# Two-pass quantised self-attention in a four-block network: where its first queries are levelled, what its shifts are formed from, and a bias for its exponentials

## The chip, the cores and the metric

The kernel runs on one core of a Trainium2 chip. A core has five engines that run side by side, each with its own instruction queue: TensorE (PE, matrix products and transposes into PSUM), VectorE (DVE), ScalarE (ACT, the activation functions), GpSimd (POOL) and SyncE (SP, which here only issues DMA). Engines wait for each other by semaphores; each works its queue in order. The metric is the device time of one execution in microseconds (us), as a median over runs.

## The reference

The network maps `x` (4096 tokens of 288 channels, here 32 tiles of 128 tokens, in 4 batches of 1024) through four blocks in a chain: block 0, a transformer block with 8-bit quantised linear layers; block 1, a cross-attention; block 2, a transformer block with fake-quantised attention; block 3, of block 0's kind. The change is mostly in block 2:

```python
def _fake_quant(x, n_bits, always_zero=False):
    levels = float(2 ** n_bits - 1)
    if always_zero:
        delta = jnp.max(x) / levels
        zp = 0.0
    else:
        xmin, xmax = jnp.min(x), jnp.max(x)
        delta = (xmax - xmin) / levels
        zp = jnp.round(-xmin / delta)
    xq = jnp.clip(_ste_round(x / delta) + zp, 0.0, levels)
    return (xq - zp) * delta

def _quant_attention(x, ctx, Wq, Wk, Wv, Wo, bo):
    q, k, v = (heads(a) for a in (x @ Wq, ctx @ Wk, ctx @ Wv))
    q, k, v = (_fake_quant(a, 8) for a in (q, k, v))
    probs = softmax(einsum('bhqd,bhkd->bhqk', q, k) / sqrt(HD))
    probs = _fake_quant(probs, 8, always_zero=True)
    return merge(einsum('bhqk,bhkd->bqhd', probs, v)) @ Wo + bo

n1 = _ln(h, ln1_g, ln1_b)
h = h + _quant_attention(n1, n1, Wq1, Wk1, Wv1, Wo1, bo1)
```

There are 16 heads of HD = 18. The minima and maxima in `_fake_quant` run over the whole tensor, all batches and heads included, so every query, key and value must exist before one of them can be quantised, and every probability before one of them can be.

## The kernel before

`x` stays on chip through all four blocks. Block 2 is `fq_attn` (L2864), which runs in four stages.

**Projection.** For each of 32 token tiles, LayerNorm (partly on POOL, lines L148 and L149), transposes, and the product with the joined Wq, Wk, Wv on TensorE (L2643, L2644); ScalarE copies the 864 results out as `y` (L3012), VectorE takes their extremes (`min_max`, L812 and L813), and `y` goes to DRAM as `raw`. In the same loop `context` prepares the keys and values of the block's cross-attention (`kq`, kT, kv, kbd), interleaved with the tiles. Then the extremes over everything become a step, its reciprocal, a zero point and a top for each of query, key and value: `global_params` (L784), called for `kq` here, for `gq` at the end of the projection, and for `qq` in the tail. Its one step across partitions is a `partition_all_reduce` on POOL (L793). `verdict` (L1201) at the end of the program and `prob_params` (L822) hold one each too.

**Pass 1** (`fq_passes`, L3030). Queries and keys are read back from `raw` (`fetch`), turned into integer levels (`fq_levels`, L819 and L820), placed with padding (`place`, L3086) and transposed on TensorE and copied by ScalarE to `qk` (`operands`, L3119). All this for batch 0 is done first: keys by VectorE, queries by POOL (`first_queries`, L3088), which runs a tile ahead of need. The loop runs over batches, head groups of four, eight query tiles and two pairs of heads: two score tiles of 128 queries x 1024 keys in PSUM (`scores_pair`, L3747), an exponential of each with its row sum (L3194, into `sums`), and one VectorE maximum over both (L3201, into `top`). The exponentials' factor is a register, `rstep`. Four tiles `e` go round between ScalarE and VectorE. Meanwhile POOL makes the levels of the next batch (`levels`, L3098). After each batch `largest` (L3148) forms 1/sums (`r`) and the largest probability of each row.

**Between the passes.** `prob_params` gives `pd`, the probabilities' step. A probability's level is exp(score) / (sums x pd), so the kernel shifts every score by -ln(sums x pd). It forms y = sums x pd (L3221), z = ln y (L3222), u = exp(-z) (L3227), and (1 - u y - z) / step, which corrects z's error once, and splits it in three bf16 parts (`log_shifts`, L3224). `add_shift` (L2541) copies a tile's parts into spare columns (POOL, L2545), transposes them (L2551), and adds them to the queries' padding rows (VectorE, L2552), where the keys hold ones. The work between the passes is in the order in which it stands in the code: 128 columns of parts, the four shifts of the first half batch, then the other 384 columns.

**Pass 2** (`attend_levels`, L3756). For 4 batches x 2 halves x 4 head groups x 8 key tiles: four score products (L3787) of keys spread block-wise in `kz` (two buffers, loaded by DMA), two exponentials of 128 x 1024 (L3796), one VectorE rounding of both to bf16 (`eb`, L3802) and four products with the values (L3770). `beside_half` weaves the output product with Wo, the next LayerNorms, the cross-attention's queries and the next half's shifts into it.

Behind it `fq_tail` does the cross-attention (its queries come back from `rawq` as `qn`) and the feed-forward. Block 3 follows; the last thing in it are `ff_stage` (L2427) and `level_residual` (L1865), whose last lines decide the program's end:

```python
y = self.wk.tile([P, C], F32, tag="y", name="y", bufs=2)
nc.vector.scalar_tensor_tensor(y, ps[:, :C], sc[:, j : j + 1], w["sw"], ALU.mult, ALU.mult)
...
nc.gpsimd.tensor_tensor(self.x[:, t, :], self.x[:, t, :], y, ALU.add)
```

Each sum of x is then stored by a DMA from SP (L2485). Along the way the kernel collects flags for values outside the range it can handle (`watch_range`, L1220); `verdict` takes the largest of them, loads it to a register, and a slower general program would run if it were not zero.

The scheduler keeps each engine's instructions nearly in the order of the code, save where `tc.issue_after(...)` sets something behind another instruction. Pools give out on-chip memory in turn, so a tile may wait until the one that lay there has been read.

Of the kernel before, what the change touches and what calls it, by code (L numbers as in the profile page):

```python
# [28 lines left out]
F32 = mybir.dt.float32  # L29
F32R = mybir.dt.float32r  # L30
BF16 = mybir.dt.bfloat16
# [6 lines left out]
P = 128  # L38
B, S, C, H, D, T, FF = 4, 1024, 288, 16, 18, 64, 1152
NTB = S // P  # L40
# [1140 lines left out]
class Fast(Net):  # L1181
# [19 lines left out]
    def verdict(self):  # L1201

        nc = self.nc
        s = self.cp.tile([P, 1], F32, name="bads")
        nc.vector.tensor_reduce(s, self.bad, AX.X, ALU.max)
        al = self.cp.tile([P, 1], F32, name="bada")
        nc.gpsimd.partition_all_reduce(al, s, P, bass_isa.ReduceOp.max)
        fl = self.cp.tile([1, 1], mybir.dt.int32, name="badi")
        nc.vector.tensor_copy(fl, al[0:1, :])
        return nc.values_load(fl[0:1, 0:1])  # L1210

    @contextmanager
# [651 lines left out]

    def level_residual(self, qT, sc, w, t, j, bias=None):  # L1865

        nc = self.nc
        ps = self.ps1()
        self.mm(ps[:, :C], qT[:, :, j * P : (j + 1) * P], w["T"], 0, C)
        y = self.wk.tile([P, C], F32, tag="y", name="y", bufs=2)  # L1870
        nc.vector.scalar_tensor_tensor(y, ps[:, :C], sc[:, j : j + 1], w["sw"], ALU.mult, ALU.mult)
        if bias is not None:
            nc.vector.tensor_tensor(y, y, bias, ALU.add)  # L1873
        nc.gpsimd.tensor_tensor(self.x[:, t, :], self.x[:, t, :], y, ALU.add)  # L1874

# [551 lines left out]
    def ff_stage(self, g3, b3, w1, w2, tops, out, m, nb, wide):  # L2427
# [5 lines left out]
        def tokens(t0):  # L2433
# [47 lines left out]
            for j in range(m):  # L2481
                t = t0 + j
                self.level_residual(fT, fc, w2, t, j)
                if out is not None:
                    nc.sync.dma_start(out[t * P : (t + 1) * P, :], x[:, t, :])  # L2485
                yield "p1.1 d.5 g.8", 0 if j + 1 < m else None
# [54 lines left out]
    def add_shift(self, qT, sp, parts, t):  # L2541


        nc = self.nc
        nc.gpsimd.tensor_copy(  # L2545
            sp[:, :, D : D + 3], parts[:, :, t * H : (t + 1) * H].rearrange("p k h -> p h k")
        )
        ps = self.ps1(BF16)
# [315 lines left out]
    def fq_attn(self, w, ctxT, beside):  # L2864
# [10 lines left out]
        with ExitStack() as es:  # L2875
# [96 lines left out]
            with (  # L2972
# [44 lines left out]
                while side:  # L3017
                    aside()
            q = self.global_params(gp, mx, nmn, "gq")

            self.watch_range(-0.5, 255.5, q["zp"], "zext")

# [7 lines left out]
    def fq_passes(self, w, q, step, raw, rawq, qmx, qmn, side, aside):  # L3030

        tc, nc = self.tc, self.nc
        with ExitStack() as es:
# [6 lines left out]
            v = gp.tile([P, NT, C + HP - D], BF16, name="v")  # L3040
            nc.gpsimd.memset(v[:, :, C:], 0.0)

            kzs = [gp.tile([P, 2, S], BF16, name="kz0")]
            spads = [gp.tile([P, H, HP], BF16, name=f"spad{n}") for n in range(2)]
# [10 lines left out]
            tp = tops.enter_context(tc.tile_pool(name="f1m", bufs=1))  # L3055
            top = tp.tile([P, NT, H], F32, name="top")
            sums = tp.tile([P, NT, H], F32, name="sums")
            r = tp.tile([P, NT, H], F32, name="rs")
            tmx = tp.tile([P, B], F32, name="tmx")
            with (  # L3060
                tc.tile_pool(name="f1l", bufs=3) as ld,
# [9 lines left out]

                def fetch(b, n, j0, m):

                    y = ld.tile([P, 3 * C], F32, tag="in", name="in")
                    y = y[:, : m * C].rearrange("p (m c) -> p m c", m=m)
                    nc.sync.dma_start(y, raw[b][:, j0 : j0 + m, n * C : (n + 1) * C])
                    return y

                def place(b, n, j, y, eng):
# [5 lines left out]
                    )  # L3085
                    eng.tensor_scalar(dst, src, q["top"][:, n : n + 1], None, ALU.min)  # L3086

                def first_queries():  # L3088

                    for j0 in range(0, NTB, 3):  # L3090
                        m = min(3, NTB - j0)
# [56 lines left out]
                def largest(b):  # L3148
# [6 lines left out]
                    nc.vector.tensor_reduce(tmx[:, b : b + 1], flat(top), AX.X, ALU.max)  # L3155

                fq0 = first_queries()
                next(fq0)
                for j0 in range(0, NTB, 3):
                    m = min(3, NTB - j0)  # L3160
                    y = fetch(0, 1, j0, m)
                    self.fq_levels(y, q, 1)
                    for j in range(m):
                        place(0, 1, j0 + j, y[:, j, :], nc.vector)
                    for j in {0: (0,), 3: (2, 4), 6: (6,)}[j0]:
                        operands(0, 1, j, 2)
                operands(0, 0, 0, 1)
                nc.gpsimd.memset(kzs[0], 0.0)
                for sp in spads:
                    nc.gpsimd.memset(sp, 0.0)  # L3170
                spare = iter(())
                for b in range(B):
                    ahead = levels(b + 1) if b + 1 < B else first_values()
                    for g in range(NG):
                        for qt in range(NTB):
# [3 lines left out]
                            with tc.issue_after(self.last) if n or b else nullcontext():  # L3179
                                if b == 0 and g == 0 and qt + 1 < NTB:  # L3180
                                    next(fq0, None)
                                    operands(0, 0, qt + 1, 1)
# [6 lines left out]
                            for pr in range(2):  # L3189
# [3 lines left out]
                                for j, sc in enumerate(scs):  # L3193
                                    nc.scalar.activation(  # L3194
                                        e[:, j, :].rearrange("p (a n) -> p a n", a=2),
# [3 lines left out]
                                        accum_out=sums[:, t, h0 + j : h0 + j + 1],  # L3199
                                    )  # L3200
                                nc.vector.tensor_reduce(top[:, t, h0 : h0 + 2], e, AX.X, ALU.max)  # L3201
                            if n in (2, 3):
                                next(spare, None)
                    if b + 1 < B:
                        with tc.issue_after(self.last):
                            both(b + 1, NTB - 1)
                    else:
                        for _ in ahead:
                            pass
                        spread(0)  # L3210
                    spare = largest(b)
                for _ in spare:
                    pass
            pd = self.prob_params(gp, tmx, "pd")
            rt = gp.tile([P, 1], F32, name="rstep")
            nc.vector.reciprocal(rt, step)
            parts = gp.tile([P, 3, NT * H], BF16, name="parts")
            flat = lambda ap: ap.rearrange("p t h -> p (t h)")
            y = flat(sums)
            z, u = (tp.tile([P, NT * H], F32, name=k) for k in ("lsz", "lsu"))  # L3220
            nc.vector.tensor_scalar(y, y, pd, None, ALU.mult)  # L3221
            nc.scalar.activation(z, y, AF.Ln)  # L3222

            def log_shifts(c0, c1):  # L3224

                yc, zc, uc = (ap[:, c0:c1] for ap in (y, z, u))
                nc.scalar.activation(uc, zc, AF.Exp, scale=-1.0)  # L3227
                nc.vector.tensor_tensor(uc, uc, yc, ALU.mult)
                nc.vector.tensor_scalar(uc, uc, -1.0, 1.0, ALU.mult, ALU.add)
                nc.vector.tensor_tensor(uc, uc, zc, ALU.subtract)  # L3230
                nc.vector.tensor_scalar(uc, uc, rt, None, ALU.mult)
                for k in range(3):
                    nc.vector.tensor_copy(parts[:, k, c0:c1], uc)
                    if k < 2:
                        nc.vector.tensor_tensor(uc, uc, parts[:, k, c0:c1], ALU.subtract)

            def shifts(b, hf):
                for j in range(hf * 4, hf * 4 + 4):
                    t = b * NTB + j
                    self.add_shift(  # L3240
                        qk[:, b, 0, :, j * P : (j + 1) * P], spads[j % 2], parts, t
                    )
                    yield

            es.enter_context(self.psum("f1o"))
            with tops:
                log_shifts(0, NTB * H)
                for _ in shifts(0, 0):
                    pass
                log_shifts(NTB * H, NT * H)  # L3250
                self.watch_range(self.R_MIN, self.R_MAX, flat(r), "wr")

            pv = gp.tile([P, 1], F32, name="pv")
            nc.vector.tensor_tensor(pv, pd, q["d"][:, 2:3], ALU.mult)
            nc.vector.tensor_scalar(wo, wo, pv, None, ALU.mult)
            at, ot, ep = pool("f1o", 1), pool("f1q", 2), pool("f1p", 2)
            kzs.append(at.tile([P, 2, S], BF16, name="kz1"))
            nc.gpsimd.memset(kzs[1], 0.0)
            g2 = self.load_bc(at, w["ln2_g"], C, "g2")
# [93 lines left out]
            def beside_half(n, oT):  # L3353

                turns = shifts(*divmod(n + 1, 2)) if n + 1 < 2 * B else iter(())
                if n:
                    for _ in range(2):
# [30 lines left out]
            for b in range(B):  # L3388
                for qh in range(2):
# [8 lines left out]

                    self.attend_levels(ep, qk[:, b, 0], keys, v, b, qh, oT, rstep, late, aside)
                    while side:  # L3400
# [354 lines left out]

    def attend_levels(self, ep, qT, keys, v, b, qh, oT, step, late, aside):  # L3756

# [22 lines left out]
        for g in range(NG):  # L3780
            kz = keys(g)
            for kt in range(NTB):
# [12 lines left out]
                for n, ps in enumerate(pss):  # L3795
                    nc.scalar.activation(e[:, 2 * n : 2 * n + 2, :], ps, AF.Exp, scale=step)  # L3796
                if len(late) > 1:
# [113 lines left out]
```

## Time and profile before

| | us |
|---|---|
| median of 3 runs | 4748.79 |
| the runs | 4748.79, 4749.89, 4741.77 |
| the profiled execution | 4740.6 |
| its span, first to last instruction | 4738.7 |
| busy in it: PE, DVE, ACT, POOL | 4183.4, 3078.2, 2992.6, 1153.8 |
| granted TensorE clock, mean | 0.88 of full speed |

Where block 2's stages lie in the profiled execution, from the timeline:

| stage | from | to |
|---|---|---|
| projection's last maximum of y | | 1716.5 |
| pass 1, first exponential to last maximum | 1732.7 | 2309.0 |
| pass 2's exponentials | 2326.4 | 2822.4 |
| cross-attention's query parameters, all-reduce | 2862.3 | |
| verdict's all-reduce; last store issued | 4722.0 | 4731.8 |

Times in the profile are us from the start of the span. A group's row reads: line, engine, operation, output<-input, sizes, how often | busy us, mean ns of one | idle us of that engine just before them, and what ended that idle time. A row of the timeline starts with its start and length, and the bracket gives the idle time before it. "issue" is time in which the engine waited for nothing that the profile shows.

### The profile page before, as it was taken

Reading aid. Unit: us, or ns where it says so; the run is one execution under the profiler, and the core shown is the slowest. Engines: PE = TensorE matmul, PEld = TensorE weight load, DVE = VectorE, ACT = ScalarE, POOL = GpSimd, SP = SyncE. Lnnn points to the kernel's source line nnn. Section 1 sums busy time; section 2 is a strip of 40 time slices with the busy share of each in tenths; the row PEclk is TensorE's granted clock in tenths of the full one; section 3 lists DMA queues with packets and bytes.
Section 4 is the critical chain, followed back from the end, with each engine's and each line's share of the span. In section 5 each row is a group of like instructions: output and inputs, shape, how many; then the busy total and the mean of one; then the engine's idle time right before and its main releaser. Section 6 shows DMA issues by size and latency. Waiting matters only on the chain. (4 is left out here: it accounts for less than half of the span.)

```text
span 4738.7 us, 62800 instructions
## 1 busy us (share of the span) xinstructions
PE 4183.4 (88%) x22827; PEld 1737.1 (37%) x22827; DVE 3078.2 (65%) x6940; ACT 2992.6 (63%) x4276; POOL 1153.8 (24%) x1742
## 2 busy tenths in 40 slices
PE   4999998889988789999789987799998999997886
PEld 2223223445566431111123333455552232223444
DVE  8355445786644779999889986545345445446885
ACT  2776776566753259999899974222215766774664
POOL 2001001333210567440023340111101000003453
PEclk9999999889999875555589998899998999998898
DMA  3000002110000321000001014002000000001000
GB/s 88 2 6 22 9 11 61 49 42 6 13 13 17 108 96 42 27 18 0 14 21 29 27 32 140 23 19 43 1 3 17 2 10 25 7 13 38 15 18 19
DMA packets 138592, 135.92 MB, mean 29 GB/s; under 512 B 69404, under 2 KB 116124, under 8 KB 136736
## 3 DMA queue, kind: packets, MB, share of 16 engines
q1 hardware_dynamic: 137072, 128.13, 9.3%
q0 software_dynamic: 1200, 3.69, 0.3%
q8 instruction: 181, 2.97, 0.3%
q14 instruction: 139, 1.14, 0.1%
HBM read 79.92 MB, written 43.47 MB: 26 GB/s over the span
## 5 line engine op out<-in xcount | busy, mean ns | idle before, releaser
L2149 ACT ACTIVATE e<-ps 128x1024 f32<-128x1024 f32 x1024 | 992.6, 1021 | 409.3 <-PE ps L2139 401.5
L2139 PE MATMUL ps<-qT,kT 32*128 32x512 f32 x4096 | 624.2, 647 | 2.7 <-DVE sext L2061 2.7
L3201 DVE TENSOR_REDUCE top<-e 128x2 f32<-128x2048 f32 x256 | 563.6, 2282 | 15.6 <-ACT e L3194 15.4
L2095 PE MATMUL ps<-e,v 128*32 128x512 f32 x4096 | 554.6, 612 | 9.1 <-DVE oT L2106 9.1
L3747 PE MATMUL ps<-qk 32*128 32x512 bf16 x1024 | 501.0, 604 | 40.4 <-ACT e L3194 38.6
L3194 ACT ACTIVATE e<-ps 128x1024 f32<-128x1024 f32 x512 | 522.0, 1192 | 6.5 <-PE ps L3747 3.1
L3796 ACT ACTIVATE e<-ps 128x1024 f32<-128x1024 f32 x512 | 476.7, 1076 | 28.7 <-PE ps L3787 15.3
L3802 DVE TENSOR_SCALAR eb<-e 128x2048 bf16<-128x2048 f32 x256 | 325.3, 1277 | 46.4 <-ACT e L3796 45.1
L1874 POOL TENSOR_TENSOR x<-x,y 128x288 f32<-128x288 f32 x192 | 152.5, 806 | 829.6 <-DVE y L1873 485.5
L2643 PE MATMUL psf<-hT,w 128*128 128x512 f32 x576 | 271.7, 594 | 0.6 <-ACT hT L2634 0.6
L2139 PEld LDWEIGHTS ps<-qT,kT 32*128 32x128 f32 x4096 | 184.7, 184 | 201.0 <-issue 128.0
L3787 PE MATMUL ps<-qk,kz 64*128 64x512 bf16 x1024 | 215.4, 422 | 31.5 <-ACT e L3796 27.3
L2095 PEld LDWEIGHTS ps<-e,v 128*32 128x32 f32 x4096 | 81.3, 108 | 403.6 <-issue 344.4
L3747 PEld LDWEIGHTS <-qk 32*128 32x128 bf16 x1024 | 53.0, 99 | 466.0 <-issue 465.0
L3670 ACT ACTIVATE gl<-psf,bf 128x512 f32<-128x512 f32 x72 | 49.4, 686 | 244.3 <-PE psf L2644 229.4
L3194 ACT ACTIVATION_READ_ACCUMULATOR e<-ps 128x1 f32 x512 | 192.4, 376 | 0.0
L1991 POOL TENSOR_TENSOR v<-y,wv1b 128x288 f32<-128x288 f32 x64 | 51.5, 810 | 562.0 <-DVE y L1988 562.0
L2106 DVE COPY oT<-ps 128x512 f32<-128x512 f32 x64 | 44.2, 690 | 213.5 <-PE ps L2095 213.5
L1489 POOL TENSOR_TENSOR h<-h,g 128x288 f32<-128x288 f32 x112 | 91.4, 817 | 362.1 <-ACT h L1486 359.6
L279 PEld LDWEIGHTS <-qT 98*128 98x128 bf16 (+2 forms) x1344 | 130.6, 103 | 125.0 <-issue 37.3
L3685 PE MATMUL psf<-w,u 128*128 128x288 f32 x576 | 147.3, 410 | 1.2 <-DVE u L3674 1.2
L3674 DVE SCALAR_TENSOR_TENSOR u<-psf,bf,gl 128x512 f32<-128x512 f32 x72 | 53.9, 749 | 144.8 <-PE psf L2644 144.7
(549 smaller groups left out, 7908.9 us busy)
## 6 DMA issues: line engine op xcount, KB each, us to landing
raw<-y SPq DMA_DIRECT2D x32, 432.0 KB
in<-raw SPq DMA_DIRECT2D x30, 432.0 KB
kz<-qk SPq DMA_DIRECT2D x128, 64.0 KB
wn<-in_L_wfc SPq DMA_DIRECT2D x12, 432.0 KB
x<-in_x SPq DMA_DIRECT2D x4, 1152.0 KB
vvo<-vt SPq DMA_DIRECT2D x16, 288.0 KB
vo<-vvo SPq DMA_DIRECT2D x4, 1152.0 KB
qn<-rawq SPq DMA_DIRECT2D x4, 1152.0 KB
```

Of the source, the lines that this page charges most:

```text
L1874: nc.gpsimd.tensor_tensor(self.x[:, t, :], self.x[:, t, :], y, ALU.add)
L2095: nc.tensor.matmul(acc[i * HP : (i + 1) * HP, :], lhsT=st["v"][:, kt, h * (D + 1) : h * (D + 1) + HP], rhs=es_[i // 2][:, i % 2, :], start ...
L2139: nc.tensor.matmul(pss[i // 2][:, i % 2, :], lhsT=self.row_tile(kT, i)[:, kt * P : (kt + 1) * P], rhs=self.row_tile(qT, i)[:, qh * 512 : ( ...
L2149: nc.scalar.activation(e, ps, AF.Exp, scale=SCALE)
L2643: nc.tensor.matmul(o, lhsT=a[:, c, :], rhs=b[:, c, :], start=(c == 0), stop=False)
L3194: nc.scalar.activation(e[:, j, :].rearrange("p (a n) -> p a n", a=2), sc, AF.Exp, scale=rstep, accum_out=sums[:, t, h0 + j : h0 + j + 1],)
L3201: nc.vector.tensor_reduce(top[:, t, h0 : h0 + 2], e, AX.X, ALU.max)
L3685: nc.tensor.matmul(ps[:, :C], lhsT=us[f][:, j * P : (j + 1) * P], rhs=w2[:, f, :], start=(f == 0), stop=(f == nf - 1),)
L3747: self.last = self.nc.tensor.matmul(ps[:, c, :], lhsT=self.row_tile(qT, i)[:, g, qt * P : (qt + 1) * P], rhs=self.row_tile(kT, i)[:, g, c ...
L3787: nc.tensor.matmul(pss[i][:, n, :], lhsT=kz[rows, i, kt * P : (kt + 1) * P], rhs=qT[rows, g, qh * 512 : (qh + 1) * 512], start=True, stop= ...
L3796: nc.scalar.activation(e[:, 2 * n : 2 * n + 2, :], ps, AF.Exp, scale=step)
L3802: nc.vector.tensor_scalar(eb, e, MAGIC, MAGIC, ALU.add, ALU.subtract)
```

## The change

It consists of five edits.

1. **Largest value over partitions.** In the fast program `global_params`, `prob_params` and `verdict` no longer use POOL: the column of per-partition values is transposed by TensorE, VectorE takes the maximum, and a product with ones hands it to all partitions. Only `gq` keeps the old form.

```diff
+    def largest_of(self, pool, s, name):
+        ps = self.ps1()
+        nc.tensor.transpose(ps[:m, :P], s, self.idf)
+        top = pool.tile([m, 1], F32, name=f"{name}c")
+        nc.vector.tensor_reduce(top, ps[:m, :P], AX.X, ALU.max)
+        row = pool.tile([m, m], F32, name=f"{name}w")
+        nc.vector.tensor_scalar(row, self.idf[:m, :m], top, None, ALU.mult)
+        ps = self.ps1()
+        nc.tensor.matmul(ps[:, :m], lhsT=self.ones[:m, :], rhs=row, start=True, stop=True)
+        return ps[:, :m]
...
     def verdict(self):
-        nc.gpsimd.partition_all_reduce(al, s, P, bass_isa.ReduceOp.max)
-        nc.vector.tensor_copy(fl, al[0:1, :])
+            nc.tensor.matmul(ps[:, 0:1], lhsT=self.ones, rhs=s, start=True, stop=True)
+            nc.vector.tensor_copy(fl, ps[0:1, 0:1])
...
-            q = self.global_params(gp, mx, nmn, "gq")
-            self.watch_range(-0.5, 255.5, q["zp"], "zext")
+            q = super().global_params(gp, mx, nmn, "gq")
```

`verdict` adds the partitions' flags up instead of taking the largest.

2. **The last four sums of x** are VectorE's.

```diff
-        nc.gpsimd.tensor_tensor(self.x[:, t, :], self.x[:, t, :], y, ALU.add)
+        eng = eng or nc.gpsimd
+        eng.tensor_tensor(self.x[:, t, :], self.x[:, t, :], y, ALU.add)
...
+                last = out is not None and t >= NT - 4
+                self.level_residual(fT, fc, w2, t, j, eng=nc.vector if last else None)
```

3. **The start of pass 1.** The first query tile is fetched alone and levelled on VectorE ahead of the keys; `first_queries` begins with tile 1, and tile 1's transposes stand behind the first pair of scores. Keys 6 and 7 go into an `e` tile. The range check of the zero points and 1/step follow the keys. The zeroing of the values' padding, of both `kz` and of the shifts' spare tiles moves behind the eighth tile of pass 1.

```diff
+                y = fetch(0, 0, 0, 1)
+                self.fq_levels(y[:, 0, :], q, 0)
+                place(0, 0, 0, y[:, 0, :], nc.vector)
+                operands(0, 0, 0, 1)
                 fq0 = first_queries()
-                next(fq0)
...
+                    if j0 == 6:
+                        y = ep.tile([P, 2, S], F32, tag="e", name="e").rearrange("p a n -> p (a n)")
...
-                operands(0, 0, 0, 1)
-                nc.gpsimd.memset(kzs[0], 0.0)
-                for sp in spads:
-                    nc.gpsimd.memset(sp, 0.0)
+                next(fq0)
+                self.watch_range(-0.5, 255.5, q["zp"], "zext")
+                nc.vector.reciprocal(rt, step)
...
+                                if b == 0 and n == 0 and pr == 0:
+                                    operands(0, 0, 1, 1)
...
+                            if b == 0 and n == NTB:
+                                with tc.issue_after(self.placed):
+                                    nc.gpsimd.memset(v[:, :, C:], 0.0)
+                                    for t in (*kzs, *spads):
+                                        nc.gpsimd.memset(t, 0.0)
```

4. **Between the passes.** The shifts are formed from the sums alone: z = ln(sums), u = exp(-z), parts of (1 - u sums - z) / step, by POOL, in pieces of 64, 64 and 384 columns. ScalarE's part follows its last exponential of pass 1 and doesn't wait for `pd`. What `pd` adds, (1 - pd exp(-ln pd)) - ln pd, is one value, `lp[:, 2:3]`. The range check of `r` follows it, and the scaling of Wo moves into `beside_half`, behind twelve of its steps.

```diff
+                with tc.issue_after(ended):
+                    nc.scalar.activation(lz, flat(sums), AF.Ln)
+                    ended = nc.scalar.activation(lu, lz, AF.Exp, scale=-1.0).ins
+                with tc.issue_after(ended):
+                    nc.scalar.activation(lp[:, 0:1], rt, AF.Ln)
+                log_parts(lz, lu, 0, NTB * H // 2)
                 for _ in spare:
                     pass
+                pd = self.prob_params(gp, tmx, "pd")
+                with tc.issue_after(self.reduced):
+                    for _ in shifts(0, 0):
+                        pass
+                nc.scalar.activation(lp[:, 0:1], pd, AF.Ln)
+                nc.scalar.activation(lp[:, 1:2], lp[:, 0:1], AF.Exp, scale=-1.0)
+                nc.vector.tensor_tensor(lp[:, 1:2], lp[:, 1:2], pd, ALU.mult)
+                nc.vector.tensor_scalar(lp[:, 1:2], lp[:, 1:2], -1.0, 1.0, ALU.mult, ALU.add)
+                done = nc.vector.tensor_tensor(lp[:, 2:3], lp[:, 1:2], lp[:, 0:1], ALU.subtract).ins
+                for c0, c1 in ((NTB * H // 2, NTB * H), (NTB * H, NT * H)):
+                    with tc.issue_after(self.copied):
+                        self.copied = log_parts(lz, lu, c0, c1)
```

5. **Pass 2's exponentials** add that value.

```diff
-                    nc.scalar.activation(e[:, 2 * n : 2 * n + 2, :], ps, AF.Exp, scale=step)
+                    nc.scalar.activation(
+                        e[:, 2 * n : 2 * n + 2, :], ps, AF.Exp, bias=bias, scale=step
+                    )
```

## The prediction

> **What bounds the kernel now.** I read the page first, then the groups of instructions with shapes kept apart, then the timeline around each place that the change touches. One core, so each stage has its own bound. The profiled execution took 4740.6 us (span 4738.7); the three timed runs have their median at 4748.79, 8.2 above. Sums are made against the profiled execution and then added to the median. About 0.2%, 9.5 us, is what a measurement of this kernel can tell from no change. The page's groups (out<-in, count, busy, mean ns, idle before):
>
> ```profile
> span 4738.7 us, 62800 instructions
> ...
> L3201 DVE TENSOR_REDUCE top<-e 128x2 f32<-128x2048 f32 x256 | 563.6, 2282 | 15.6 <-ACT e L3194 15.4
> ...
> L3796 ACT ACTIVATE e<-ps 128x1024 f32<-128x1024 f32 x512 | 476.7, 1076 | 28.7 <-PE ps L3787 15.3
> L3802 DVE TENSOR_SCALAR eb<-e 128x2048 bf16<-128x2048 f32 x256 | 325.3, 1277 | 46.4 <-ACT e L3796 45.1
> ```
>
> In block 2, pass 1 is bound by VectorE's 256 maxima (11.1 of the 15.6 idle us are before the first), pass 2 by ScalarE's 512 exponentials. The timeline gives the borders of both passes and one undisturbed run of pass 2 (start, length, what, count, idle before):
>
> ```profile
> 1738.03 24.83 DVE L3201 TENSOR_REDUCE top<-e 128x2 f32<-128x2048 f32 x11 [11.09 <-ACT e L3194]
> ...
> 2309.03 0.96 DVE L3152 RECIPROCAL rs<-sums 128x128 f32<-128x128 f32 x1
> ...
> 2326.41 3.77 ACT L3796 ACTIVATE e<-ps 128x1024 f32<-128x1024 f32 x4 [9.39 <-PE ps L3787]
> ...
> 2396.96 26.20 ACT L3796 ACTIVATE e<-ps 128x1024 f32<-128x1024 f32 x28 [0.58 <-PE ps L3787]
> ```
>
> Pass 1 thus runs from the first maximum at 1738.03 to 2309.03, a gap of 17.4 us follows, and pass 2 runs from 2326.41 to 2822.4, 496 us. In the run of 28 the exponentials follow each other every 0.9326 us (26.20 less the last one's 1.02, over 27); 512 of them make 477.5, so 18.5 of the 496 us are ScalarE waiting. The windows of pass 2 (PE, PEld, DVE, ACT, POOL busy, then clock, DMA):
>
> ```profile
> 2510.00:2570.00 60.00, 54.27 (x337) 20.21 (x335) 54.05 (x81) 58.25 (x64) 25.08 (x20) 0.97 0.10 28
> ```
>
> TensorE and VectorE are at 54 of 60: close behind ScalarE, but behind.
>
> **Part 1: the largest value over partitions moves from POOL to TensorE and VectorE.** The timeline at two of POOL's all-reduces, each with POOL's next tensor operation:
>
> ```profile
> 1625.07 0.39 POOL L793 PARTITION_ALL_REDUCE kqr<-kqs  x1 [5.59 <-issue]
> ...
> 1632.62 0.79 POOL L149 TENSOR_TENSOR h<-h,b 128x288 f32<-128x288 f32 x1 [7.16 <-issue]
> ...
> 4721.95 0.38 POOL L1207 PARTITION_ALL_REDUCE bada<-bads  x1 [5.86 <-issue]
> ...
> 4729.48 2.28 POOL L1874 TENSOR_TENSOR x<-x,y 128x288 f32<-128x288 f32 x3 [7.16 <-issue]
> ```
>
> Each costs POOL 5.6 to 5.9 us before and 7.2 after it. The Trainium skill (GPSIMD Engine Reference, section 2.1, Instruction dispatch) has a freshly loaded kernel's first call pay about 6 us. By this rule removing one saves 6 us; by the rows it saves 13, because the way back costs again. I take the rows.
>
> *End.* The last sum of x waits for the way back: POOL's three adds end at 4731.76, the last store is issued at 4731.8. In the new kernel the last four adds are VectorE's, by another such add there about 0.45 us. TensorE's last product ends at 4721.07, the last y takes 0.52, so x is ready at about 4722.1 and the store goes out 9.6 us earlier. By the rule's 6 us it would be 4.5 less; I take 9.6 (9 to 10.5). The verdict's matmul and copy (under 1 us) end beside it.
>
> *Keys' parameters, in the projection.* While POOL is away, the LayerNorm steps it does are missing and TensorE starves (PE, PEld, DVE, ACT, POOL, clock, DMA):
>
> ```profile
> 1610.00:1620.00 10.00, 9.09 (x34) 5.37 (x33) 8.48 (x16) 3.30 (x8) 3.95 (x5) 1.00 0.22 90
> 1620.00:1630.00 10.00, 6.40 (x20) 3.41 (x18) 7.11 (x20) 2.48 (x4) 0.39 (x1) 0.92 0.33 133
> 1630.00:1640.00 10.00, 3.98 (x9) 1.90 (x10) 9.84 (x13) 0.88 (x4) 6.63 (x8) 0.50 0.00 0
> 1640.00:1650.00 10.00, 6.13 (x15) 3.04 (x14) 9.91 (x15) 1.18 (x7) 9.27 (x11) 0.67 0.38 158
> ```
>
> The copies of y (L3012), every 3.7 us on average, come at 1626.48 and then at 1649.99: 23.5 instead of 3.7, 19.8 us lost. Not all returns. In the new order the transpose of the keys' extremes stands five matmuls into a pair of tokens and waits for VectorE, whose extremes end at 1618.4; TensorE would be there at about 1613.9, 4.3 us of waiting. And VectorE did some 10 us of key quantising and casts inside the stall; outside it finds about 1.5 us free in 10, so I estimate half of it on the path. 19.8 - 4.3 - 5 = 10 (4 to 16).
>
> *Queries and probabilities in the tail.* The queries' all-reduce ran at 2862.26 after 9.33 us of POOL's load; their first level step at 2864.37. The new chain would be ready near 2855.7, but then qn's load decides: issued at 2853.50 behind about 2 MB, I estimate its first tile at 2861 to 2862.5. Gain 2.5 (1 to 4). The tail's second reduction, at 2967.41, found POOL ready: reduce plus reaction took 0.6; transpose, maximum, product and matmul take about 1.2. Net gain here 1.9.
>
> **Part 2: start of pass 1.** The chain before: POOL returns from its all-reduce at 1725.34, levels query 0, with two memsets (0.46, 1.80) between, ends at 1730.31; transpose, copy, first scores, first exponential 1732.72; the second waits for POOL's next queries and starts only at 1736.88; first maximum 1738.03. Now query 0 is levelled on VectorE, the memsets are moved behind eight tiles of pass 1 (POOL has room there), and the last two keys no longer wait 1.45 us for a buffer. But query 1 stays with POOL, and TensorE's queue holds its transposes ahead of the second half of the first scores. POOL: 1725.34 + 0.5 + 1.25 + 1.0 with queueing behind query 2's first step gives 1729.8; transposes and copy 1.0, so the first exponential at about 1731.1, the second 1 us on, the first maximum at 1733.2. Gain 4.9 (2 to 6).
>
> **Part 3: the gap between the passes.** Before: 17.4 us of maxima, all-reduce, two table loads of 1.28, logarithm, VectorE's parts, shifts. Now the logarithm of the sums, its exponential and the warm-up logarithm run on ScalarE at 2302.57, when its last pass-1 exponential ended, 6.5 us ahead of VectorE, so three loads are covered; the first 64 columns' parts are formed by POOL in that cover (about 1.9 us to spare). What remains after 2309.03, from the same rows: reciprocal 0.96, product 0.3, maxima 0.3 and 0.15 (with dispatch 1.6 in all); transpose 0.37, maximum 0.3, diagonal 0.2, matmul 0.35, scale 0.19; Ln 0.24, table load 1.28, Exp 0.2; four short VectorE steps with the shift adds (0.42 each) and one 0.68 range check woven in, about 2.2; scores 0.6. About 7.7 us: gain 9.7 (7 to 11). POOL's remaining parts (448 columns, an estimated 8 to 9 us) lie before the second half's shifts, needed some 30 us later; the new position of kz1's memset and of Wo's scaling is inside pass 2 too, where POOL is busy 25 of 60.
>
> **Part 4: the bias of pass 2's exponentials, a price.** The 512 exponentials had a scale from a register and no bias; now each reads a bias pointer. Groups of the same shape and source, one with a pointer and one without:
>
> ```profile
> L2377 ACT ACTIVATE ec<-ps,kb 128x512 f32<-128x512 f32 x128 | 82.6, 689 | 39.4 <-PE ps L2374 27.9 <-DMA wfc1sw<-sw1d 10.8
> L3617 ACT ACTIVATE ec<-ps 128x512 f32<-128x512 f32 x64 | 34.3, 598 | 125.1 <-PE ps L3613 109.2 <-POOL spad L2545 11.2 <-DVE ebc L3619 4.6
> ```
>
> 689 against 598: 91 ns. Back to back, too: pairs of L2377 take 1.27, a spacing of 0.58; L3617's eight in a row take 4.03, 0.49. That is 0.086 to 0.093 per instruction, not hidden by overlap. The rule that speaks against this change: the Trainium skill (ScalarE: Activation LUTs, section What ACT_TABLE_LOAD costs) prices each pointer operand at about 93 ns over 186 + 0.833 N, with 93 ns overlap between neighbours. By it 1024 columns have a spacing of 1.039 and 512 take 532; by the rows 0.9326 + 0.0885 = 1.021, 512 take 523, 45.3 more than now. I take the rows. Against it stand the 18.5 us of waits: 10.9 of them were for VectorE's eb and the rest for TensorE, both 10% faster than the new pace needs, so most go. I let 14 go, since the first shifts and the low clock (0.61 in 2330 to 2390) keep some: 45.3 - 14 = 31 (27 if all go, 45 if none).
>
> **Sum.** Gains 10 + 9.6 + 1.9 + 4.9 + 9.7 = 36.1; price 31; net -5.1: 4735.5 in a profiled execution, 4744 beside the median. Inside what can be told from no change.
>
> **Rivals.** (a) *Waits and stall both swallowed*: all 18.5 us of waits go (price 27) and the projection returns 16 (gains 42): -15, 4734. For it: VectorE and TensorE have 10% to spare, and the queue's order can hide the 4.3 us. Against it: VectorE in the projection is 78 to 85% busy. (b) *Slower*: pass 2's waits are of order, not of rate (an exponential that finds its e buffer or its scores late stays late at any pace), so the price is the whole 45 to 47; and VectorE's work in the projection gives back only 4 of the stall (gains 30): +15 to 17, 4765. With the gains at 36 it decides from a price of 45.6, with 30 from 39.6. For it: waits sit after single pairs of exponentials in the trace (0.4 to 0.6 us, some on eb, some on scores). (c) *The gap does not shrink as said*: POOL's parts come late for the first shift, or another table load falls on the path; gap 12 in place of 7.7, net -1, 4748.
>
> **Chances.** Forecast 0.39 (own range 4737 to 4752; 0.06 of it faster, 0.33 the same). (a) 0.33: 0.32 faster, 0.01 the same. (b) 0.20: 0.19 slower, 0.01 the same. (c) 0.08: 0.05 the same, 0.03 slower. Faster 0.38, same 0.40, slower 0.22. The range reaches from two thirds into (a), 4724, to most of (b), 4763.
>
> **What would show it.** Pass 2's exponentials at about 1.10 to 1.17 us mean and pass 2 near 527 us (price); ScalarE's idle in it under 5 us; the first one about 7.7 us after the last maximum's end; the first maximum of pass 1 some 5 us earlier after the global all-reduce; the y copies around the keys' parameters at most 14 us apart; the last store issued within 1 us of the last product. Wrong would be: a pass 2 that stays near 500, which would make it faster by some 30; or one of 540.

## The result: slower, by pass 2 alone

The changed kernel takes 4785.54 us (median of 4 runs, 4774.58 to 4790.13), the kernel before 4747.48 (4 runs): a ratio of 1.0076, 95% interval 1.0064 to 1.0088. That is 38 us more, outside the range that was given. The profiled executions differ by 46.1 us, and the timeline lets that be put down to stages (us of the profiled executions):

| stage | before | after | change |
|---|---|---|---|
| start to the last extremes of the projection | 1716.5 | 1714.8 | -1.7 |
| from there to pass 1's first maximum | 21.5 | 16.9 | -4.6 |
| pass 1, first maximum to last | 571.0 | 570.7 | -0.3 |
| gap between the passes | 17.4 | 8.4 | -8.9 |
| pass 2, first exponential to last | 496.0 | 563.1 | **+67.1** |
| to the first level step of the tail's queries | 42.0 | 38.9 | -3.0 |
| from there to TensorE's last product | 1856.7 | 1862.7 | +6.0 |
| from there to the end | 17.6 | 9.2 | -8.4 |

So the gains came, all but the projection's, and pass 2 took more than all of them. (The 6.0 us in the tail are no more than such profiles differ by; see the part on why the prediction was wrong.) The page's groups of the changed kernel, as shown for the kernel before (line, engine, operation, count, then busy, mean ns, then idle time and what ended it):

```profile
span 4784.8 us, 62835 instructions
...
L3278 DVE TENSOR_REDUCE top<-e 128x2 f32<-128x2048 f32 x256 | 563.5, 2277 | 12.5 <-ACT e L3271 12.3
...
L3869 ACT ACTIVATE e<-ps,lp 128x1024 f32<-128x1024 f32 x512 | 524.7, 1134 | 41.3 <-PE ps L3860 23.3
...
L3877 DVE TENSOR_SCALAR eb<-e 128x2048 bf16<-128x2048 f32 x256 | 322.9, 1263 | 79.9 <-ACT e L3869 79.3
```

`lp` is the new bias, which each exponential reads through a pointer (one value for each partition); it is called the pointer below. The exponential's mean is 1134 ns where it was 1076: that was foreseen. The idle time before it is not: it was to fall and rose from 28.7 to 41.3 us, although 6.4 us of the old idle time, ScalarE's wait in the gap, are gone from it (the bracket below has 2.99 where 9.39 stood). The timeline:

```profile
1731.69 29.32 DVE L3278 TENSOR_REDUCE top<-e 128x2 f32<-128x2048 f32 x13 [8.20 <-ACT e L3271]
...
2302.40 0.94 DVE L3224 RECIPROCAL rs<-sums 128x128 f32<-128x128 f32 x1
...
2310.85 20.30 ACT L3869 ACTIVATE e<-ps,lp 128x1024 f32<-128x1024 f32 x20 [2.99 <-PE ps L3860]
...
2416.92 36.32 ACT L3869 ACTIVATE e<-ps,lp 128x1024 f32<-128x1024 f32 x36 [0.60 <-DVE mvk L3357]
```

The pace of the exponentials shows in stretches in which none comes late, here one of the kernel before and one of the changed kernel:

```profile
2514.41 22.11 ACT L3796 ACTIVATE e<-ps 128x1024 f32<-128x1024 f32 x24
...
2435.05 18.19 ACT L3869 ACTIVATE e<-ps,lp 128x1024 f32<-128x1024 f32 x18
```

They follow each other every 0.905 us before ((22.11 - 1.29) / 23, the last one's length taken off) and every 0.998 us after ((18.19 - 1.23) / 17). Over the whole of pass 2 the median distance from one start to the next is 0.905 and 0.997 us, 0.092 more. 512 of them make 463.4 and 510.5 us; what is left of the 496.0 and 563.1 us are waits, 32.6 before and 52.6 after. So the 67.1 us are 47.1 of pace and 20.0 of new waits.

The whole of pass 2, first before, then after (PE, PEld, DVE, ACT, POOL busy, then clock, DMA share, GB/s):

```profile
2326.41:2822.41 496.00, 446.58 (x2618) 159.52 (x2617) 427.80 (x607) 476.67 (x512) 168.77 (x140) 0.90 0.09 26
...
2310.85:2873.91 563.06, 481.37 (x2619) 168.55 (x2615) 431.58 (x611) 524.71 (x512) 152.89 (x152) 0.83 0.09 23
```

TensorE does the same products in 481 us in place of 447, at a mean clock of 0.83 in place of 0.90. In these traces the clock is either 1.00 or 0.50, so it is at half for 195 of 563 us, where it was for 97 of 496. Counted by the clock of the moment in which they arise, 27.6 of the 52.6 us of waits fall in time at half clock (10.2 of 32.6 before); at full clock there are 24.9 (22.4 before). So 17 of the 20 us of new waits lie where TensorE's clock is at half. One window of 60 us:

```profile
2510.00:2570.00 60.00, 52.34 (x288) 18.95 (x286) 46.37 (x69) 55.88 (x55) 19.32 (x20) 0.86 0.07 19
```

TensorE is busy for nearly as long as before (54.27), but with 288 products in place of 337, at a granted clock of 0.86 in place of 0.97. Cut into stretches of 4 us, the same view shows the order of things:

```profile
2440.00:2444.00 4.00, 2.51 (x20) 0.93 (x20) 3.09 (x5) 4.00 (x5) 1.14 (x1) 1.00 0.01 3
2444.00:2448.00 4.00, 2.35 (x16) 0.77 (x16) 2.44 (x3) 4.00 (x5) 0.00 (x0) 0.93 0.13 33
2448.00:2452.00 4.00, 3.40 (x16) 0.68 (x16) 2.21 (x3) 4.00 (x5) 0.00 (x0) 0.50 0.14 35
2452.00:2456.00 4.00, 3.24 (x11) 1.20 (x11) 2.93 (x4) 3.53 (x5) 0.00 (x0) 0.50 0.00 0
2456.00:2460.00 4.00, 4.00 (x20) 1.32 (x20) 2.02 (x2) 3.31 (x4) 0.00 (x0) 0.79 0.00 0
```

For 8 us ScalarE works without a pause and TensorE, ahead of it, is busy for only 2.4 of 4 us, since nothing but scores and values is in its queue there, and each pair of scores waits for ScalarE to free its PSUM tile:

```profile
2444.25 0.39 PE L3860 MATMUL ps<-qk,kz 64*128 64x512 bf16 x2 [0.61 <-ACT e L3869]
2444.57 0.40 PE L3843 MATMUL ps<-eb,v 128*32 128x512 bf16 x4
2445.25 0.39 PE L3860 MATMUL ps<-qk,kz 64*128 64x512 bf16 x2 [0.28 <-ACT e L3869]
2446.26 0.39 PE L3860 MATMUL ps<-qk,kz 64*128 64x512 bf16 x2 [0.61 <-ACT e L3869]
```

Then TensorE's clock goes to 0.50, and with products woven in again ScalarE has gaps (3.53, 3.31 of 4). Another such stretch in the timeline of the changed kernel (start, length, engine, line, count), at half clock and ten us later at the full one:

```profile
2403.18 1.33 PE L3341 MATMUL ps<-wo,oT 128*128 128x288 f32 x2
...
2404.44 0.61 PE L3860 MATMUL ps<-qk,kz 64*128 64x512 bf16 x2
...
2405.09 2.20 ACT L3869 ACTIVATE e<-ps,lp 128x1024 f32<-128x1024 f32 x2 [0.69 <-PE ps L3860]
...
2411.61 0.75 PE L3341 MATMUL ps<-wo,oT 128*128 128x288 f32 x2
...
2413.63 0.39 PE L3860 MATMUL ps<-qk,kz 64*128 64x512 bf16 x2
```

At 2403 two products with Wo take 1.33 us and two score products 0.61; then 0.75 and 0.39. At half clock the products woven in come between ScalarE and its scores, and it waits 0.69 us.

### The profile page after: what moved, and what is told of

Read it like the earlier page. It is cut to its first block, busy times and chain, and to the rows that moved or that the text cites. A ratio compares the mean times of both kernels' runs of the same rounds, so it can differ in the third digit from the quotient of the medians.

```text
span 4784.8 us, 62835 instructions
## 1 busy us (share of the span) xinstructions
PE 4220.5 (88%) x22841; PEld 1750.1 (37%) x22841; DVE 3078.4 (64%) x6941; ACT 3043.0 (64%) x4280; POOL 1131.5 (24%) x1757
## 5 line engine op out<-in xcount | busy, mean ns | idle before, releaser
L2196 ACT ACTIVATE e<-ps 128x1024 f32<-128x1024 f32 x1024 | 992.5, 1021 | 410.1 <-PE ps L2186 402.3
L3869 ACT ACTIVATE e<-ps,lp 128x1024 f32<-128x1024 f32 x512 | 524.7, 1134 | 41.3 <-PE ps L3860 23.3
L3271 ACT ACTIVATE e<-ps 128x1024 f32<-128x1024 f32 x512 | 521.5, 1190 | 5.6 <-PE ps L3820 2.0
L279 PEld LDWEIGHTS <-qT 98*128 98x128 bf16 (+2 forms) x1344 | 129.5, 103 | 123.9 <-ACT qT L1437 37.1
L3843 PE MATMUL ps<-eb,v 128*32 128x512 bf16 x1024 | 118.2, 451 | 36.9 <-DVE eb L3877 35.0
```

What stands on the lines that cost most here:

```text
L279: self.nc.tensor.matmul(out, lhsT=lhs[:, k, :], rhs=rhs[:, k, c0:c1], start=(k == 0), stop=(k == kc - 1))
L2196: nc.scalar.activation(e, ps, AF.Exp, scale=SCALE)
L3271: ended = nc.scalar.activation(e[:, j, :].rearrange("p (a n) -> p a n", a=2), sc, AF.Exp, scale=rstep, accum_out=sums[:, t, h0 + j : h0 + ...
```

## The experiments

Two theories went in. **A**: the pointer slows ScalarE, TensorE then idles more, its clock falls, and its slower products make ScalarE wait. **B**: the new waits come from the other edits of pass 2 (what is woven in, and in which order). A third, **C**, came with the fifth run: that the pointer's own reads do it, not the pace. Each run's profile gives pass 2's length, its pace (512 times the median distance between exponentials), the waits (the length less the pace; in brackets those at half clock) and the mean clock in pass 2. The last column looks at the order of TensorE's products in the trace: it counts stretches of three or more key tiles in a row with nothing woven in between their scores and values.

| run | ratio to before, 95% interval | pass 2, us | pace, us | waits, us | clock | plain stretches |
|---|---|---|---|---|---|---|
| before | 1 | 496.0 | 463.4 | 32.6 (10.2) | 0.90 | 3 |
| changed kernel | 1.0076 (1.0064 to 1.0088) | 563.1 | 510.5 | 52.6 (27.6) | 0.83 | 18 |
| before, pointer alone | 1.0116 (1.0099 to 1.0133) | 549.9 | 510.5 | 39.4 (18.7) | 0.85 | 17 |
| changed, no pointer | 0.9953 (0.9937 to 0.9970) | 500.0 | 462.8 | 37.1 (11.6) | 0.92 | 4 |
| changed, step in padding | 0.9961 (0.9947 to 0.9975) | 501.6 | 463.4 | 38.3 (13.7) | 0.90 | 4 |
| changed, one product more | 1.0012 (1.0005 to 1.0019) | 528.1 | 510.0 | 18.2 (1.9) | 0.97 | 4 |
| padding, one product more | 0.9968 (0.9956 to 0.9981) | 501.8 | 463.4 | 38.4 (2.5) | 0.98 | 4 |
| before, slower pace, no pointer | 1.0061 (1.0043 to 1.0079) | 521.9 | 486.7 | 35.3 (16.3) | 0.88 | 3 |

How far single profiles differ: seven runs without pointer and at full pace have waits of 32.6 to 39.1 us and a clock of 0.90 to 0.92; the changed kernel and the run with its keys on POOL, whose pass 2 is the same, have 52.6 and 44.5 us, at 0.83 and 0.84.

**The pointer alone, in the kernel before.**

```diff
+            zb = gp.tile([P, 1], F32, name="zb")
+            nc.vector.memset(zb, 0.0)
...
-                    self.attend_levels(ep, qk[:, b, 0], keys, v, b, qh, oT, rstep, late, aside)
+                    self.attend_levels(ep, qk[:, b, 0], keys, v, b, qh, oT, rstep, zb, late, aside)
...
-                    nc.scalar.activation(e[:, 2 * n : 2 * n + 2, :], ps, AF.Exp, scale=step)
+                    nc.scalar.activation(
+                        e[:, 2 * n : 2 * n + 2, :], ps, AF.Exp, bias=bias, scale=step
+                    )
```

> The kernel before, and only pass 2's exponentials get a bias pointer (to a column of zeros). Theory A (pointer and clock): the pointer alone makes all of pass 2's loss, 1.006 us from one exponential to the next in place of 0.933 (+37.6 us), and as ScalarE's slower pace leaves TensorE idle more often, its granted clock in pass 2 falls from 0.97 to about 0.87, its products take longer and ScalarE's waits rise from 18.5 to 45 to 50 us: pass 2 about 560 us, time 4747 + 66 = 4813. Theory B (the other edits of pass 2, the order of what is woven in, make the waits): the waits shrink to 5 to 18 us, pass 2 about 525, clock 0.95 or more, time 4765 to 4785.

Measured: 4799.99 us, 51.7 more than before. Pass 2 is 53.9 us longer with not one other edit: 47.1 of pace and 6.8 of waits. The clock is 0.94 from 2510 to 2570, but 0.78 in the 60 us before:

```profile
2450.00:2510.00 60.00, 50.04 (x269) 16.44 (x267) 45.92 (x64) 56.09 (x56) 22.05 (x20) 0.78 0.07 17
```

A's time was too large by 13 us, B's too small by 15 at the least. The clock falls to 0.85 without the other edits, and the waits don't shrink, so those edits aren't needed for it; that the waits grew by 6.8 is hardly more than single profiles differ by.

One thing is not separated here. TensorE's products in pass 2 stand in another order than before, although a bias of ScalarE's was all that was edited: the scheduler's "nearly in the order of the code" leaves room for that. The order is nearly the changed kernel's (17 plain stretches, 18 there, 3 before). So the pointer comes with a slower ScalarE and with an order in which woven-in products stand in clumps, and no run has one of them without the other and nothing else changed.

**The changed kernel without the pointer, and with the step in another place.** The first leaves the step's factor out. The second computes all that the reference asks: the step's logarithm goes as three more bf16 parts into padding columns of the queries, over ones in the keys.

```diff
-                    nc.gpsimd.memset(pd[:, 1, :, D : D + 3], 1.0)
+                    nc.gpsimd.memset(pd[:, 1, :, D : D + 6], 1.0)
...
+                for sp in spads:
+                    done = nc.vector.tensor_copy(
+                        sp[:, :, D + 3 : D + 6], lb.unsqueeze(1).to_broadcast([P, H, 3])
+                    ).ins
...
-                        e[:, 2 * n : 2 * n + 2, :], ps, AF.Exp, bias=bias, scale=step
+                        e[:, 2 * n : 2 * n + 2, :], ps, AF.Exp, scale=step
```

> The changed kernel without the pointer in pass 2: the factor of the probabilities' step is left out of the exponentials. Theory A: pass 2 back at about 496 us with a clock near 0.97, and all the gains stand: 4785 - 67 = 4718. Theory B: the waits stay near 48 us, pass 2 about 525, time 4747.

> The changed kernel, with the probabilities' step not as a bias but as three more bf16 parts in spare padding columns of the queries (the keys hold ones there), so pass 2's exponentials have no pointer; the first shifts wait for the step, so the gap between the passes grows from 8.4 to about 11 us. Theory A: pass 2 about 496, time 4720, faster than both kernels. Theory B: about 4749.

Measured: 4726.20 and 4726.82. Pass 2 is back at 500.0 and 501.6 us, so the pointer, with the order that comes with it, was worth 63 of the changed kernel's 67 us there. A's times, 4718 and 4720, were 8 and 7 us too low, B's 21 and 22 too high. The gap between the passes is 11.2 us with the padding columns, and that version beats both kernels: 0.9961 of before. The group of its exponentials has no pointer and the old mean again:

```profile
L3880 ACT ACTIVATE e<-ps 128x1024 f32<-128x1024 f32 x512 | 477.3, 1076 | 30.0 <-PE ps L3871 14.1 <-DVE eb L3888 12.7 <-DVE lnt L1507 1.2
```

**More work for TensorE.** This run was to separate work from clock: the pointer stays, and TensorE gets one product of zeros more for 7 of 8 key tiles.

```diff
+                if i == 0 and kt < NTB - 1:
+                    for _ in range(1):
+                        nc.tensor.matmul(
+                            acc[i * HP : (i + 1) * HP, :], lhsT=self.none, rhs=eb[:, i, :],
+                            start=False, stop=False,
+                        )
```

> The changed kernel, with one product more for each key tile of pass 2 (zeros added to the accumulator of the values, 7 of 8 tiles): more work for TensorE, nothing else. Theory A in its strong form (idle time takes the clock down, and a busier TensorE keeps it up): the clock in pass 2 at 0.93 or more, ScalarE's waits down from 48 to 20 to 35 us, time 4757 to 4775. If TensorE's queue itself is too full (work, not clock): waits and time up, 4790 to 4815.

Measured: 4753.64, 31.9 us less than the changed kernel, by doing more, and better than A's 4757 to 4775. The clock is 0.97 over pass 2, 1.00 in the window, and the waits fall to 18.2 us:

```profile
2510.00:2570.00 60.00, 54.55 (x340) 19.38 (x335) 51.87 (x77) 59.14 (x59) 22.99 (x20) 1.00 0.09 24
```

```profile
L3877 ACT ACTIVATE e<-ps,lp 128x1024 f32<-128x1024 f32 x512 | 518.2, 1179 | 12.9 <-PE ps L3868 6.0 <-DVE eb L3885 5.2 <-DVE mvk L3359 1.1
```

In the window TensorE now does 340 products in 54.55 us, where it had 288 in 52.34. What is left of pass 2's loss, 528.1 against 496.0, is 46.6 us of the pointer's pace less 14.4 of waits. The clock stayed up and the waits went, nearly all of those at half clock (1.9 us are left). The run doesn't show what kept the clock up: the order of the products changed here too, and with it the plain stretches went from 18 back to 4. With the step in padding columns the same product brings nothing:

> The step in padding columns (no pointer) and the extra product for each key tile. Theory A, weak form (at ScalarE's full pace TensorE keeps its clock by itself): clock 0.97 to 1.0, pass 2 490 to 502, time 4715 to 4727, within 10 us of the version without the extra product. If the extra work is on the path there: 4735 to 4755.

Measured: 4729.57, pass 2 at 501.8 us. The clock did rise, from 0.90 to 0.98, and the waits at half clock fell from 13.7 to 2.5 us; but those at full clock rose from 24.5 to 35.8. That fits a TensorE which, at ScalarE's full pace, has no room for one product more; no run tests this by itself.

**A slower pace without a pointer.** The first try put a copy of one column behind each two exponentials:

```diff
+                nc.scalar.copy(self.zb[:, 1:2], self.zb[:, 0:1])
```

> The kernel before with one copy of a single column on ScalarE after each two exponentials of pass 2: no pointer, only a slower pace, by an estimated 0.1 to 0.2 us for two. Theory A (any slower pace of ScalarE takes TensorE's clock down): clock in pass 2 at 0.92 or less from 2450 on, ScalarE's waits above the 18.5 us of before, pass 2 at 535 to 565 us, time 4785 to 4815. Theory C (the pointer's own reads do it, not the pace): clock stays near 0.97, the waits shrink, pass 2 at 500 to 525, time 4752 to 4777.

Measured: 4760.61, ratio 1.0028 (1.0019 to 1.0037), and nothing on the question. The copies depended on nothing in pass 2, so the scheduler placed them in pass 1, where they cost some 10 us (581.0 in place of 571.0). The second try reads the exponentials' own output:

```diff
+                nc.scalar.copy(self.zb[:, 1:2], e[:, 3, 511:512])
```

> The kernel before with one copy of a single column of e on ScalarE behind each two exponentials of pass 2 (it reads what they wrote, so it stays there): a slower pace by an estimated 0.1 to 0.3 us for two, no pointer. In the earlier try the copies had no input from pass 2 and went into pass 1. Theory A (any slower pace takes TensorE's clock down): clock at 0.92 or less from 2450 on, pass 2 at 540 us or more, time 4790 or more. Theory C (the pointer's own reads): clock near 0.97, pass 2 longer by no more than the copies' own time less the waits, 500 to 530, time 4752 to 4780.

Measured: 4774.88. Two exponentials and a copy take 1.901 us (medians of 0.916 and 0.985) in place of 1.810: 0.091 for two, half of the pointer's price for each. That makes 23 us of pace; pass 2 grew by 25.9. The waits, 35.3 us, lie inside the 32.6 to 39.1 of the runs at full pace: they neither shrank nor clearly grew. The clock fell a little, to 0.88, with 16.3 us of waits at half clock, more than any of those seven runs has. The times are in C's ranges, not in A's. So TensorE's clock falls without a pointer too, at half the slowing by less than A said; that the pointer's reads add to it is not excluded. The order of TensorE's products changed in this run as well (15 stretches of two plain key tiles, 8 before).

**The keys' parameters in the projection.**

```diff
-                kq.update(self.global_params(gp, kmx, knm, "kq"))
+                kq.update(Net.global_params(self, gp, kmx, knm, "kq"))
```

> The changed kernel with the keys' parameters in the projection back on POOL's all-reduce. By the forecast (a gain of 10 from this step): 4795. By the trace of the changed kernel (the stall moved to VectorE's queue, 1.3 us won): 4785 to 4788.

Measured: 4781.69, ratio 1.0081 (1.0065 to 1.0098), not to be told from the changed kernel (1.0076): in the projection the edit that this run takes back brought nothing that can be told, where 10 us were forecast. The copies of y, first to last, take 145.6 us before, 144.3 after, 145.2 in this run. The timeline of the changed kernel shows POOL at the place of its old reload:

```profile
1622.96 0.98 POOL L148 TENSOR_TENSOR h<-h,g 128x288 f32<-128x288 f32 x1 [10.59 <-DVE kqrd L1240]
```

POOL is free and idle for 10.59 us; it waits for VectorE, which has the extremes and the key chain in its queue ahead of the LayerNorm step that POOL needs. Two runs asked whether it is the order or the work:

> The version with the step in padding columns, and the keys' parameters in the projection cut into pieces over six tokens instead of two: the transpose stands behind a whole pair of products, the levels go in halves. If VectorE's queue order and TensorE's wait on it eat the gain there (the trace of the changed kernel): 8 to 15 us less than without it, 4712 to 4719. If the 10 us of VectorE's key work are on the path in any order: 4722 to 4730.

> The version with the step in padding columns, without VectorE's work on the cross-attention's keys and values in the projection: their levels, the first set of casts and the values' tiles are left out (some 10 us of VectorE). If this work is what takes the place of POOL's stall: the projection ends 7 to 12 us earlier, 4715 to 4720 for the whole. If TensorE's waits and its low clock do it: within 4 us of the version with it, 4723 to 4731.

Spreading the chain over six tokens: 4729.64, ratio 0.9963 (0.9949 to 0.9977), no gain over 4726.82, and the copies of y took 146.7 us. Leaving VectorE's key work out: 4717.24, ratio 0.9937 (0.9920 to 0.9953), the copies of y 135.0 us, 9.2 less than with it. So VectorE's work was the bound in both orders tried.

**The end alone, in the kernel before** (verdict and the last four sums as in the change):

> The kernel before with only the end changed: verdict through TensorE and the last four sums on VectorE. By the forecast 9.6 us less, 4738. If the stores' landing takes over: 6 or less, 4742.

Measured: 4737.84, ratio 0.9980 (0.9970 to 0.9990), 8.6 us less, as forecast within a us. In the changed kernel, which ends the same way, the last sum is made right behind the last y:

```profile
4775.63 0.52 DVE L1917 SCALAR_TENSOR_TENSOR y<-ps,sc,wfc2sw 128x288 f32<-128x288 f32 x1 [1.01 <-PE ps L279]
4776.18 0.46 DVE L1921 TENSOR_TENSOR x<-x,y 128x288 f32<-128x288 f32 x1
```

## Why the prediction was wrong

**The step that failed** is in the fourth part: "Against it stand the 18.5 us of waits: 10.9 of them were for VectorE's eb and the rest for TensorE, both 10% faster than the new pace needs, so most go." It took TensorE's speed as given. The forecast let 14 us of waits go; they rose by 20.0 (32.6 to 52.6), 17 of these in time in which TensorE's clock was at half. With the clock at 0.97 instead of 0.83, in the run with one product more, 14.4 us did go, and pass 2 took 528.1 us, where 527 was forecast. So the sum was right for a TensorE of constant speed. That 14 was met so closely is in part luck, since the waits to begin with were 32.6 us and not 18.5.

That size came from a run of 28 exponentials, 0.9326 us apart, taken as undisturbed. It wasn't: two of them come late, by 0.29 and 0.36 us. The timeline shows no break there, since neighbours overlap in the profile (an exponential stands there for 1.02 to 1.29 us, and the next one starts after 0.905), so that lateness leaves little idle time or none. A median over all distances does not have this fault.

Why the clock fell further is only in part shown. The window over 60 us that was looked at, at 0.97, could not tell, since what decides are stretches of a few us (last section). A hint was there: the low stretch at 0.61 from 2330 to 2390 was named, and only used to keep 4 us of waits.

**The pointer's own price** was right: 0.0885 us for each was forecast and 0.092 measured, 47.1 us in place of 45.3. The Trainium skill's 93 ns for a pointer operand (ScalarE: Activation LUTs, What ACT_TABLE_LOAD costs) holds for the distance between neighbours here too; its formula as a whole gave a distance of 1.039 us, and 0.997 was measured.

**Rival (b)** had the right side, and the price of 45 to 47 with nothing of it absorbed. It kept the waits as they were, where they grew by 20 us, and its 4765 was 20 us short. Its cause, waits that stay at any pace, did not hold: in the run with one product more they shrank.

**The gains**, forecast and measured: gap between the passes 9.7 and 8.9; start of pass 1 4.9 and 4.6; end 9.6 and 8.4 (8.6 alone); tail queries 2.5 and 2.3 (11.9 us from the last extremes to the first level step before, 9.6 after, the last wait being for qn's load, as said). The projection's 10 was 0 to 1.3. The term that failed there is "I estimate half of it on the path" for VectorE's key work: all of it was, 9.2 us in the run that left it out. (The other copies of y come every 4.1 us on average, not 3.7, so 19.4 us were lost to the stall.) Of the 5.9 us that 19.4 - 4.3 - 9.2 leaves, at most 1.3 came; where the rest went is open.

**The tail.** The stretch from the tail's queries to the last product is 6.0 us longer in the changed kernel's profile. That can't be called a loss: with the tail as before it takes 1852.6 to 1864.3 us in five runs, with the new one 1855.9 to 1864.0 in eight.

**Open** is what parts the pointer alone (549.9 us of pass 2) from the whole change (563.1): the run with the keys on POOL, with the same pass 2 as the change, had 555.0, so much of it is scatter. Open above all is whether the slower pace or the new order of TensorE's products took the clock down. A run with the pointer alone and TensorE's order held as it was would tell.

## What to carry over

TensorE, running just ahead of the bound, has its speed only as long as its work is spread evenly: before the bound engine is slowed on purpose, look at TensorE's clock in windows of a few us, and count its products at half clock too. Compare the order of the products as well: an edit on one engine can move another's instructions. In a pass that ScalarE bounds, a constant for all elements of a score tile belongs in a padding row of the product's operands, where it cost 2.8 us once, not in a pointer read by each of 512 activations. And when an engine's stall is removed, count what the other engines did during it: their work doesn't go away with the stall.

## What the hardware showed

In pass 2 of all 13 traces TensorE's clock keeps one value for 3.413 us or a multiple of it. Cut into such steps, the time at full clock shows what takes the clock down: each of the 56 steps in which TensorE was busy for less than 57% was followed by half clock, none of the 1326 with 70% or more was, and of the 174 between these, 87 were. In the changed kernel there were 19 falls; TensorE was busy for 44 to 70% of the step ahead of each, and in 17 of these steps it did scores and values alone, with nothing woven in. The mean over a whole pass says little: the changed kernel has TensorE busy for 85% of pass 2 at a clock of 0.83, the run with one product more for 88% at 0.97, the kernel before for 90% at 0.90.

The Trainium skill (TensorE: Matmul & The Clock Gate, What's actually happening) lowers the clock after an idle window of about 3.4 us. Here no idle window was needed: the clock fell to 0.50 at 2447.4 after 8 us in which TensorE was busy for 60% of the time, and no idle time of TensorE in the timeline from 2436 to 2447 is longer than 0.61 us. The same page's section on psum-queue depth-cycling, short pauses between groups of products, is nearer to what these windows show.

A bias pointer made each exponential of 1024 columns 0.092 us dearer. And work added to an engine that is not the bound, in an order that changed with it, made the kernel 31.9 us faster.
